# Layer 0 begun pair by pair, its second pair of images made between the passes, and group-norm statistics by batch-norm instructions: a four-layer convolution stack on one core

## The chip, the cores and the metric

The kernel runs on one core of a Trainium2 chip. The metric is the device time of one launch in microseconds. Before the change it is 3129.97 us, the median of three runs (3129.84 to 3130.12).

## What is computed

The input is four images of 32 x 32 pixels with 16 channels. Three layers of one kind follow each other, and then one of another kind; each adds its result to what it was given.

```python
def _gn(v, G=8, eps=1e-5):              # mean and variance over (32, 32, C/8) of one image
    ...
def conv(inputs, M, Wp, G):             # layers 0 to 2
    first   = einsum('ijpq,bpqc->bijc', M2, inputs)
    shifted = conv3x3(inputs, K)        # K: a 3x3x16 filter for every (i, j, f)
    diff    = relu(inputs[:, :, :, None, None, :] - shifted)
    second  = einsum('ijpq,bpqijc->bijc', W2, diff)
    return first - second
x = x + conv(_gn(x), M0, W0, G0)        # layer 0; layers 1 and 2 alike
x = x + conv(...)
x = x + conv(...)
x = x + layer3(_gn(x), ...)             # a rational filter, applied as a product with Toeplitz blocks
```

## The kernel before

**Tiling.** The 1024 output pixels of a layer, times 16 filters, are cut into NBLK = 128 blocks of 128 columns. One *unit* of work is one block of one image: ten matmul instructions at L472 (six products in two row halves: `ga` and `gb` in float32, which take two instructions each, and `gn` in float32r) fill one two-bank PSUM buffer, and one VectorE instruction at L480 (`junk`) takes the minimum with zero, multiplies with the weights `wt` and sums into `acc`. There are four PSUM buffers, so TensorE can be at most four units ahead of VectorE. A layer has 512 units, the three layers 1536.

**Order.** `conv_layer` writes the order out by hand as jobs. In layers 1 and 2 the first eight blocks are two jobs, one for images 0 and 1 and one for images 2 and 3; in layer 0 they are one job over all four images (L448). The last eight blocks are again two jobs. A chunk is GC = 8 blocks of G. `load_g` loads a chunk (`ga`, `gb` in two halves of rows each, and the broadcast `g9`); `prepare_g` subtracts on GpSimd (L400), casts `g9` to `gn` on ScalarE (L404) and forms two low parts on VectorE (L407). `load_w` (L411) loads the weights of two blocks, 1024 KB on the SP queue, as a broadcast of 8 rows to 128 partitions; only the very first such tile comes ready-made from `w0`. There are six weight buffers.

After every unit `step()` (L427) advances the generators in `todo`, so that the instructions of a generator stand between units in the order of each engine. All engines work through their instructions in the order in which they are written.

**Start of layer 0.** The host sends three shifted copies per pair of images (`raw`); `load_first(a, which, queue)` loads one of them for pair `a`, 544 KB: two into the images `ims[a][0]`, `ims[a][1]` and one into `nine[a]`. `first_images` (L168) runs the group norm on all four images, and from it makes the images in place: `center` (ScalarE, L177) subtracts the mean, `clear` (GpSimd memsets, L195) zeroes the borders, `scale` (ScalarE, L181) and `first_tap` (VectorE, L199) multiply by 1/std, and `last_tap` (VectorE, L204 to L206) makes the third image from `nine`. All four images are made before the first unit's L480. The chunk 0 of G is loaded and prepared in two parts, `halves`: blocks 0 and 1 first, blocks 2 to 7 after. The second part is prepared by the generator `rest`: its subtraction at the first step, its cast and low parts (`list(second)`, L248) at the eighth.

The SP queue carries, in this order: x, raw of pair 0, `ga`, `ga` (first part), raw of pair 1 twice, w0, the second part of chunk 0 (`ga`, `gb`, `ga`, `gb`, `g9`), weights tile 1, chunk 1 of G (1.5 MB), and further weights tiles.

**Group norm** (L104 to L145), in all layers: sum on VectorE (L110), group sum by a small matmul against `avg` (L101), mean (L114, L116), centred copy `xc` (L120), square (L125), sum (L127), group sum again, then 1/std (L132 to L144). `normalise` (L256) multiplies `xc` by 1/std. In layers 1 and 2 it runs as a generator (`make_image`) beside units, one pair at a time; before layer 3 it is `norm3` (L745), which for the second pair has the Toeplitz products of the first pair (L729) issued around its steps.

Of the kernel before, what the change touches and what calls it, by code (L numbers as in the profile page):

```python
# [37 lines left out]
P = 128  # L38
# [5 lines left out]
GC = 8  # L44
# [10 lines left out]
def conv_stack_kernel(ctx, tc, x, raw, w0, M, W, G, den, num, h0, cst, dft, one, idp, idq, perm, out):  # L55
# [40 lines left out]
    def group_sums(s):  # L96

        pt = pair_psum()
        for h in range(2):
            rows = slice(64 * h, 64 * h + 64)  # L100
            nc.tensor.matmul(pt[:, h, : s.shape[1]], lhsT=avg[rows], rhs=s[rows], start=True, stop=True)  # L101
        return [pt[:, h, : s.shape[1]] for h in range(2)]

    def group_norm(xt, center=None, sums=group_sums):  # L104


        nb = xt.shape[1]
        vec = lambda name: small.tile([P, B], F32, tag=name, name=name)[:, :nb]
        s = vec("s")
        nc.vector.tensor_reduce(s, xt, AX.X, ALU.add)  # L110
        yield
        pm = sums(s)
        mean = vec("mean")
        nc.vector.tensor_copy(mean, pm[0])  # L114
        for more in pm[1:]:
            nc.vector.tensor_tensor(mean, mean, more, ALU.add)  # L116
        if center:
            center(mean)
        xc = work.tile([P, B, NBLK], F32, tag="xc", name="xc")[:, :nb]
        nc.vector.tensor_tensor(  # L120
            xc, xt, mean.unsqueeze(2).to_broadcast([P, nb, NBLK]), ALU.subtract
        )
        sq = junkp.tile([P, S * S], F32, tag="junk", name="sq")[:, : nb * NBLK]
        sq = sq.rearrange("p (b n) -> p b n", b=nb)
        nc.vector.tensor_tensor(sq, xc, xc, ALU.mult)  # L125
        ss = vec("ss")
        nc.vector.tensor_reduce(ss, sq, AX.X, ALU.add)  # L127
        yield
        yield
        pv = sums(ss)  # L130
        v = vec("v")
        nc.vector.tensor_scalar(v, pv[0], 1e-5, None, ALU.add)  # L132
        for more in pv[1:]:
            nc.vector.tensor_tensor(v, v, more, ALU.add)

        r = vec("r")
        nc.scalar.activation(r, v, AF.Sqrt)
        ri = vec("ri")
        nc.vector.reciprocal(ri, r)
        nc.vector.tensor_tensor(ri, ri, v, ALU.mult)  # L140
        nc.vector.tensor_tensor(r, r, ri, ALU.add)
        nc.vector.tensor_scalar(r, r, 0.5, None, ALU.mult)
        rstd = vec("rstd")
        nc.vector.reciprocal(rstd, r)  # L144
        return xc, rstd  # L145

    over = lambda v: v.unsqueeze(2).to_broadcast([P, v.shape[1], NBLK])
# [20 lines left out]
    def first_images():  # L168

        of = lambda t, b: t[:, :, b % 2].rearrange("p l cc x -> p l (cc x)")  # L170
        neg = st.tile([P, B], F32, name="neg")
# [29 lines left out]
        def last_tap(b):  # L201

            v, v8, m = of(nine[b // 2], b), of(ims[b // 2][2], b), neg[:, b : b + 1]
            nc.vector.tensor_scalar(v8, v, m, rstd[:, b : b + 1], ALU.add, ALU.mult)  # L204
            nc.vector.tensor_scalar(v, v, m, rlo[:, b : b + 1], ALU.add, ALU.mult)
            nc.vector.scalar_tensor_tensor(v8, v8.bitcast(F32), sign, v, ALU.mult, ALU.add)  # L206
            clear(2, b // 2, slice(b % 2, b % 2 + 1))

        first = prepare_g(0, 0, halves[0])

        def early(mean):
            nc.vector.tensor_scalar(neg, mean, -1.0, None, ALU.mult)
            center(0, 0, 1)
            clear(0, 0)
            next(first)

        norm = group_norm(xs, early)
        while True:
            try:
                next(norm)  # L220
            except StopIteration as end:
                xc, rstd = end.value
# [6 lines left out]
        last_tap(0)  # L229
        list(first)  # L230
        scale(1)
        center(0, 2, 3)
        clear(0, 1)
        first_tap(1)
        last_tap(1)
        center(1, 2, 3)
        clear(1, 1)
        for b in (2, 3):
            scale(b)
            first_tap(b)  # L240
            last_tap(b)

        def rest():
            second = prepare_g(0, 0, halves[1])
            next(second)
            for _ in range(6):
                yield
            list(second)  # L248
            yield
            for a in range(2):  # L250
                normalise(a, xc[:, 2 * a : 2 * a + 2], rstd[:, 2 * a : 2 * a + 2])
                yield
# [3 lines left out]
    def normalise(a, xc, rstd):  # L256
        yc[a] = work.tile([P, 2, NBLK], F32, tag=f"yc{a}", name=f"yc{a}")
        nc.vector.tensor_tensor(yc[a], xc, over(rstd), ALU.mult)

    def make_image(a, xt):  # L260

        xc, rstd = yield from group_norm(xt[:, 2 * a : 2 * a + 2])
        store_image(a, xc, rstd)
# [3 lines left out]
    def store_image(a, xc, rstd):  # L267
        split = lambda t: t.rearrange("p b (cc q) -> p b cc q", q=S)
        whole, hi, lo = (ys[a][:, k, :, :, 1:33] for k in range(3))
        normalise(a, xc, rstd)  # L270
# [163 lines left out]
    def conv_layer(layer, xt, finish, side=(), also=iter(())):  # L434
# [12 lines left out]

        jobs = [(range(GC), (0, 1)), (range(GC), (2, 3))] if layer else [(range(GC), range(B))]  # L448
        jobs += [(range(blk, blk + GC), range(B)) for blk in range(GC, NBLK - GC, GC)]
        jobs += [(last, (0, 1)), (last, (2, 3))]  # L450
        for job, (blks, batches) in enumerate(jobs):
            pairs = layer and job < 2, job >= len(jobs) - 2
            for k, blk in enumerate(blks):
# [8 lines left out]
                if (job or not layer) and k == 6:  # L462
# [27 lines left out]
                if not any(pairs) and layer + job:  # L490
# [157 lines left out]
    with tc.tile_pool(name="st", bufs=1) as st:  # L648
# [17 lines left out]
        load_first(1, 0, nc.sync)  # L666
        load_first(1, 1, nc.sync)
        load_first(1, 2, nc.gpsimd)
# [3 lines left out]
        list(load_g(0, 1))  # L672
        load_w()
        first_images()
        load_w()
# [69 lines left out]
    def norm3(a, xt):  # L745
        stats = []

        def column_sums(s):
# [4 lines left out]
            pt = stats[0][:, column_sums.n, :nb]  # L753
# [4 lines left out]
            return [pt]  # L758
# [19 lines left out]
        xc, rstd = yield from steps  # L778
        if a:
            run(early[2])  # L780
        for y in (
# [3 lines left out]
            nc.vector.tensor_tensor(  # L785
                y.rearrange("p cc q b -> p b cc q"),
                xc.rearrange("p b (cc q) -> p b cc q", q=S),
                over(rstd).rearrange("p b (cc q) -> p b cc q", q=S),
                ALU.mult,
            )  # L790
# [175 lines left out]
```

## Time and profile before

| | us |
|---|---|
| median of three runs | 3129.97 |
| the profiled execution | 3129.71 |
| span of its profile, first to last instruction | 3127.8 |
| TensorE busy in it | 3109.3 |
| VectorE busy | 2069.8 |
| ScalarE busy | 82.2 |
| GpSimd busy | 233.4 |

The profile's page gives for each engine its busy time and its share of the span. A group line names the source line, the engine, the operation and the tiles, written as output<-inputs. In the timeline each row has a start, a length, the engine and the line; a bracket at its end says how long the engine had been idle before it and what ended that idle time. `PEld` is TensorE's loading of stationary operands, which overlaps its matmuls. The windows give the busy time of each engine in a stretch, and after it TensorE's granted clock, the mean busy share of the 16 DMA engines and the rate in GB/s.

### The profile page before, as it was taken

What the parts mean: (1) busy time and instruction counts of PE and PEld (TensorE: products, weight loads), DVE (VectorE), ACT (ScalarE), POOL (GpSimd) and SP (SyncE); (2) the same over time, 40 slices, a digit from 0 to 9 for tenths busy, and PEclk for the clock granted to TensorE, in tenths of its full rate; (3) what the DMA queues carried; (4) which work ended last, traced back from release to release, by engine and by line L of the source; (5) the groups of instructions that cost most, each with busy time, mean ns of one, the idle gap of its engine ahead of it and who ended that gap; (6) DMA issues with size and microseconds to landing.
All of it is one profiled execution on the core that took longest, in us unless ns stands there. A gap on an engine that the chain in (4) does not pass through costs nothing.

```text
span 3127.8 us, 39384 instructions
## 1 busy us (share of the span) xinstructions
PE 3109.3 (99%) x16312; PEld 1703.7 (54%) x16312; DVE 2069.8 (66%) x3318; ACT 82.2 (3%) x107; POOL 233.4 (7%) x259
## 2 busy tenths in 40 slices
PE   8999999999999999999999999999999999999999
PEld 4445567777777554455445455455455454455444
DVE  7666666666667766666666666766666666666663
ACT  1000000000000000000000000000000000000000
POOL 1002321000000100100000000010010000000000
PEclk9999999999999999999999999999999999999999
DMA  6553344333342665433333343266544444444511
GB/s 192 150 119 91 87 115 111 98 88 87 97 98 69 129 148 123 99 86 87 98 98 88 87 97 98 68 131 148 127 106 101 99 105 106 102 97 106 112 38 22
DMA packets 67599, 321.35 MB, mean 103 GB/s; under 512 B 10058, under 2 KB 17100, under 8 KB 41948
## 3 DMA queue, kind: packets, MB, share of 16 engines
q1 hardware_dynamic: 56776, 300.62, 40.1%
q10 hardware_dynamic: 6484, 10.81, 1.7%
q0 software_dynamic: 4160, 7.40, 1.2%
q8 instruction: 128, 2.10, 0.3%
q14 instruction: 51, 0.42, 0.1%
HBM read 313.16 MB, written 5.63 MB: 102 GB/s over the span
## 4 chain that ended last, share of the span: by engine, by line
PE 99%; DVE 1%; DMA 0%; POOL 0%; issue 0%; ACT 0%; DVEq 0%; POOLq 0%
PE pt L472 96%; PE pt L729 2%; PE pt L326 1%; DVE junk L480 0%; DMA gb<-in_G_dram 0%; PE pt L525 0%; PE pt L568 0%; DMA cs<-in_cst_dram 0%; PE pt L607 0%; POOL im L195 0%; PE pt L101 0%; DVE x L495 0%; DVE s L110 0%; PE pt L314 0%; ACT im L181 0%
## 5 line engine op out<-in xcount | busy, mean ns | idle before, releaser
L480 DVE SCALAR_TENSOR_TENSOR junk<-pt,w 128x1024 f32<-128x1024 f32 x1536 | 1880.9, 1225 | 992.8 <-PE pt L472 973.9
L472 PE MATMUL pt<-im,ga 64*128 64x512 f32 x6144 | 1679.4, 591 | 3.1 <-POOL ga L400 3.1
L472 PE MATMUL pt<-im,gb 64*128 64x512 f32 x6144 | 1671.7, 588 | 0.7 <-ACT im L181 0.7
L472 PE MATMUL pt<-im,gn 64*128 64x512 f32 x3072 | 1345.9, 806 | 0.0
L472 PEld LDWEIGHTS pt<-im,gb 64*128 64x128 f32 x6144 | 687.5, 185 | 655.9 <-issue 575.4
L472 PEld LDWEIGHTS pt<-im,ga 64*128 64x128 f32 x6144 | 680.4, 187 | 378.6 <-DVE junk L480 230.1
L472 PEld LDWEIGHTS pt<-im,gn 64*128 64x128 f32 x3072 | 356.1, 186 | 325.6 <-issue 286.7
L400 POOL TENSOR_TENSOR ga<-ga,cs 128x1024 f32<-128x1024 f32 (+2 forms) x49 | 113.5, 2317 | 2119.2 <-DMA ga<-in_G_dram 2118.1
L480 DVE DVE_READ_ACCUMULATOR junk<-pt,w 128x1 f32 x1536 | 127.4, 83 | 0.0
L407 DVE TENSOR_TENSOR gn<-g,gn 32x1024 fp32r<-32x1024 f32 (+2 forms) x98 | 120.4, 1229 | 5.1 <-ACT gn L404 3.0
L404 ACT CAST gn<-g 128x1024 fp32r<-128x1024 f32 (+2 forms) x49 | 50.4, 1029 | 2348.7 <-DMA g<-in_G_dram 2086.4
L350 POOL DMA_DIRECT2D fd<-ft x48 | 25.1, 530 | 231.0 <-DVE ft L343 213.5
L860 DVE TENSOR_TENSOR xo<-xo,pt 32x512 f32<-32x512 f32 x5 | 3.4, 682 | 35.8 <-PE pt L729 35.7
L729 PE MATMUL pt<-t,y 128*32 128x512 f32 (+3 forms) x352 | 24.3, 433 | 0.8 <-DVE xo L860 0.8
L326 PE MATMUL pt<-mt,yt 128*64 128x512 f32 x96 | 21.9, 598 | 0.0
L729 PEld LDWEIGHTS pt<-t,y 128*32 128x32 f32 x352 | 11.9, 110 | 13.5 <-issue 9.9
L292 POOL DMA_DIRECT2D im<-img x32 | 16.2, 513 | 8.9 <-DMA img<-y 8.8
L326 PEld LDWEIGHTS pt<-mt,yt 128*64 128x64 f32 x96 | 6.3, 136 | 13.7 <-issue 9.4
L729 PE MATMUL pt<-t,yp 128*32 128x512 f32 (+3 forms) x192 | 13.4, 434 | 0.0
L546 POOL TENSOR_TENSOR H<-H,d 128x256 f32<-128x256 f32 (+1 forms) x10 | 8.2, 822 | 68.1 <-DVE d L551 67.7
L275 POOL COPY e<-y 32x612 f32<-32x612 f32 x4 | 2.8, 692 | 120.6 <-DVE y L274 120.6
L546 POOL TENSOR_TENSOR t<-s 128x256 f32<-128x256 f32 (+1 forms) x15 | 11.3, 755 | 0.0
(94 smaller groups left out, 209.6 us busy)
## 6 DMA issues: line engine op xcount, KB each, us to landing
w<-in_W_dram SPq DMA_DIRECT2D x191, 1024.0 KB
ga<-in_G_dram SPq DMA_DIRECT2D x94, 256.0 KB
gb<-in_G_dram SPq DMA_DIRECT2D x94, 256.0 KB
g<-in_G_dram SPq DMA_DIRECT2D x47, 512.0 KB
mt<-in_M_dram SPq DMA_DIRECT2D x24, 512.0 KB
t<-hd ACTq DMA_DIRECT2D x28, 160.0 KB
t<-hd SPq DMA_DIRECT2D x28, 160.0 KB
im<-img SPq DMA_DIRECT2D x32, 67.5 KB
```

What stands on the lines that cost most here:

```text
L275: nc.gpsimd.tensor_copy(ye[a][96:, :, :, 1:, :], ys[a][96:, :, :, :3, :])
L292: (nc.sync, nc.scalar, nc.gpsimd)[n % 3].dma_start(out=ims[a][k][at : at + C] .bitcast(F32) .rearrange("c l b cc x -> c l (b cc x)")[:, :, ...
L326: nc.tensor.matmul(pf[64 * h : 64 * h + 64], lhsT=yt[:, 4 * part + k].rearrange("k b c -> k (b c)"), rhs=mts[k][:, h, :], start=(k == 0), ...
L350: nc.gpsimd.dma_start(out=fv[h, cc, b], in_=ft[at : at + C, cc])
L400: nc.gpsimd.tensor_tensor(gv, gv, mid.unsqueeze(1).to_broadcast([P, gv.shape[1], C]), ALU.subtract)
L404: nc.scalar.copy(gn, g9)
L407: nc.vector.tensor_tensor(lo, g9[r : r + 32], lo.bitcast(F32), ALU.subtract)
L472: nc.tensor.matmul(pt[:, half, :], lhsT=w[rows, blk % GC, :], rhs=im[rows, :, b % 2, :, :S], start=n == 0, stop=n == 2,)
L480: nc.vector.scalar_tensor_tensor(junk, pt.rearrange("p h m -> p (h m)"), 0.0, wt, ALU.min, ALU.mult, accum_out=acc[b // 2][:, b % 2, blk : ...
L546: mul = lambda o, u, w: nc.gpsimd.tensor_tensor(o, u, w, ALU.mult)
L729: nc.tensor.matmul(rows[:, :, r], lhsT=lhsT, rhs=rhs, start=at not in begun, stop=left[at] == 0)
L860: nc.vector.tensor_tensor(row, row, src, ALU.add)
```

## The change

Layer 0 now begins like the other layers, with two jobs for the first eight blocks: images 0 and 1, then images 2 and 3. The raw copies of pair 1 are all loaded on the SP queue, behind weights tiles 1 and 2. Chunk 1 of G is loaded inside the first job. The images of pair 1 are made by `rest`, between units: the cast and low parts of the second part of chunk 0 at the second step, centring and clearing of pair 1 at the third, image 2 at steps 8 to 11, image 3 at steps 12 to 15, and `normalise` at 16 and 17. In all layers the statistics come from VectorE's `bn_stats`, one instruction per image, which gives means and squared deviations of even and odd elements; three small instructions form the group's squared deviation, and no centred copy is kept. `normalise` and the end of `norm3` become one two-scalar instruction per image.

```diff
     def group_norm(xt, center=None, sums=group_sums):
-        s = vec("s")
-        nc.vector.tensor_reduce(s, xt, AX.X, ALU.add)
+        st = small.tile([P, B, 2, 3], F32, tag="st", name="st")[:, :nb]
+        for b in range(nb):
+            nc.vector.bn_stats(st[:, b].rearrange("p e k -> p (e k)"), xt[:, b])
+        half, m, m2 = NBLK // 2, st[:, :, :, 1], st[:, :, :, 2]
         yield
-        pm = sums(s)
-        mean = vec("mean")
-        nc.vector.tensor_copy(mean, pm[0])
-        for more in pm[1:]:
-            nc.vector.tensor_tensor(mean, mean, more, ALU.add)
+        pm, axes = sums(m)
+        neg = vec("neg")
+        nc.vector.tensor_reduce(neg, pm, axes, ALU.add)
+        nc.vector.tensor_scalar(neg, neg, -float(half), None, ALU.mult)
         if center:
-            center(mean)
-        xc = work.tile([P, B, NBLK], F32, tag="xc", name="xc")[:, :nb]
-        nc.vector.tensor_tensor(
-            xc, xt, mean.unsqueeze(2).to_broadcast([P, nb, NBLK]), ALU.subtract
-        )
...
-        nc.vector.tensor_tensor(sq, xc, xc, ALU.mult)
-        ss = vec("ss")
-        nc.vector.tensor_reduce(ss, sq, AX.X, ALU.add)
+            center(neg)
+        d = small.tile([P, B, 2], F32, tag="d", name="d")[:, :nb]
+        nc.vector.tensor_tensor(d, m, neg.unsqueeze(2).to_broadcast([P, nb, 2]), ALU.add)
+        nc.vector.tensor_tensor(d, d, d, ALU.mult)
+        nc.vector.scalar_tensor_tensor(d, d, float(half), m2, ALU.mult, ALU.add)
...
-        first = prepare_g(0, 0, halves[0])
+        first, second = (prepare_g(0, 0, part) for part in halves)
...
         first_tap(0)
         nc.vector.tensor_scalar(rlo, rstd, is_lo, None, ALU.mult)
-        last_tap(0)
+        list(last_tap(0))
         list(first)
         scale(1)
-        center(0, 2, 3)
-        clear(0, 1)
         first_tap(1)
-        last_tap(1)
-        center(1, 2, 3)
-        clear(1, 1)
-        for b in (2, 3):
-            scale(b)
-            first_tap(b)
-            last_tap(b)
+        list(last_tap(1))
+        next(second)
 
         def rest():
-            second = prepare_g(0, 0, halves[1])
-            next(second)
-            for _ in range(6):
-                yield
+
+            yield
             list(second)
             yield
+            for which in range(2):
+                center(which, 2, 3)
+                clear(which, 1)
+            yield
+            for _ in range(4):
+                yield
+            for b in (2, 3):
+                scale(b)
+                first_tap(b)
+                yield
+                yield from last_tap(b)
+                yield
             for a in range(2):
...
-        jobs = [(range(GC), (0, 1)), (range(GC), (2, 3))] if layer else [(range(GC), range(B))]
+        jobs = [(range(GC), (0, 1)), (range(GC), (2, 3))]
...
-            pairs = layer and job < 2, job >= len(jobs) - 2
+            pairs = job < 2, job >= len(jobs) - 2
...
         next(loads)
         next(loads)
-        load_first(1, 0, nc.sync)
-        load_first(1, 1, nc.sync)
-        load_first(1, 2, nc.gpsimd)
         load_w()
         list(loads)
         load_w()
-        list(load_g(0, 1))
+        load_w()
+        for which in range(3):
+            load_first(1, which, nc.sync)
         load_w()
         first_images()
-        load_w()
```

`last_tap` yields after each of its first two VectorE instructions. `normalise` becomes, per image, `tensor_scalar(yc[a][:, b], xt[:, b], neg[:, at], rstd[:, at], ALU.add, ALU.mult)`.

## The prediction

> **What bounds the kernel now.** I read the page's busy times first, then the chain of work that ended last in order of time, then what TensorE waits for, then the timeline of the first 60 us and of the ends of the layers.
>
> ```profile
> PE 3109.3 (99%) x16312; PEld 1703.7 (54%) x16312; DVE 2069.8 (66%) x3318; ACT 82.2 (3%) x107; POOL 233.4 (7%) x259
> ```
>
> TensorE is busy for all but 18.5 us. Nothing in the change takes a matmul away from L472, so it can win only in those 18.5 us, and lose wherever TensorE is made to wait. The waits it has:
>
> ```profile
> PE pt L101 <- DVE s L110: 6.9, 6, 4.9
> PE pt L472 <- POOL ga L400: 3.1, 1, 3.1
> PE pt L101 <- DVE ss L127: 3.0, 2, 2.7
> PE pt L472 <- ACT im L181: 0.7, 2, 0.4
> ```
>
> Columns: us in total, times, longest. The longest ones are the start; what is left is about 0.4 us at each of five pair ends. The start, from the timeline:
>
> ```profile
> 11.06 0.72 POOL L400 TENSOR_TENSOR ga<-ga,cs 128x256 f32<-128x256 f32 x1 [1.02 <-DMA gb<-in_G_dram]
> ...
> 19.56 1.06 PE L472 MATMUL pt<-im,ga 64*128 64x512 f32 x4
> ...
> 20.98 1.13 PE L472 MATMUL pt<-im,gb 64*128 64x512 f32 x4 [0.36 <-ACT im L181]
> ...
> 24.14 1.04 PE L472 MATMUL pt<-im,ga 64*128 64x512 f32 x4
> ...
> 27.58 0.83 ACT L404 CAST gn<-g 128x768 fp32r<-128x768 f32 x1 [6.01 <-DMA g<-in_G_dram]
> ...
> 31.59 1.93 DVE L407 TENSOR_TENSOR gn<-g,gn 32x768 fp32r<-32x768 f32 x2
> ...
> 35.66 1.23 DVE L480 SCALAR_TENSOR_TENSOR junk<-pt,w 128x1024 f32<-128x1024 f32 x1 [0.54 <-DMA w<-in_W_dram]
> ...
> 39.03 2.36 POOL L400 TENSOR_TENSOR ga<-ga,cs 128x1024 f32<-128x1024 f32 x1 [14.31 <-DMA ga<-in_G_dram]
> ```
>
> ```profile
> 52.33 1.23 DVE L480 SCALAR_TENSOR_TENSOR junk<-pt,w 128x1024 f32<-128x1024 f32 x1 [3.18 <-DMA w<-in_W_dram]
> ```
>
> Three things are to be seen. The first matmul waits for a piece of chunk 0 that lands at 11.06. The third unit starts at 19.56 and the fifth at 24.14; the rows after repeat every 1.963 us (26.11, 28.07, 30.03), so two periods from 19.56 would give 23.49: image 2 cost 0.65. And three brackets date landings: the second part of `g9` at 27.58, weights tile 1 at 35.66, tile 2 at 52.33. Tile 2 came 3.18 us late for VectorE, and TensorE did not stop: four PSUM buffers cover nearly three units.
>
> ```profile
> 4.00:8.00 4.00, 0.59 (x4) 0.51 (x4) 3.03 (x7) 0.33 (x1) 0.00 (x0) 1.00 1.03 402
> 12.00:16.00 4.00, 3.71 (x10) 1.44 (x10) 2.89 (x7) 2.60 (x5) 1.39 (x8) 1.00 1.02 418
> 28.00:34.00 6.00, 6.00 (x35) 3.23 (x34) 5.70 (x9) 0.41 (x1) 0.00 (x0) 1.00 0.52 130
> 70.00:78.00 8.00, 8.00 (x42) 4.06 (x40) 5.57 (x9) 0.00 (x0) 0.00 (x0) 1.00 0.51 211
> ```
>
> The last two columns are the DMA engines' share and GB/s. While raw copies move, all 16 engines are busy at 402 to 418. While only a weights tile moves, half of them are, at 130: 35.66 - 27.58 = 8.1 us per tile. Later (70 to 78) a tile runs at 211, 5.0 us.
>
> [...] The weights' source has 8 outermost, and the share of 0.52 agrees. [...] `ga` of chunk 1, queued on SP behind tile 1, let L400 start only at 39.03, after tile 1. [...] rows here agree (4 elements 161 ns, 256 elements 426, 512 elements 691). [...]
>
> **The change, part by part.** *Start, first two units.* The piece awaited at 11.06 stands ahead of pair 1's raw copies on its queue before and after, so I put nothing there; the earlier 1/std buys nothing either, since memsets and L400 come later. Third unit without image 2's wait: **-0.65**. TensorE's undisturbed schedule is then unit n at 19.56 + 1.963(n-3): unit 5 at 23.49, 9 at 31.34, 13 at 39.19, 17 at 47.04, 19 at 50.97.
>
> *What the transfers allow.* The first job has two images instead of four, so half as much work covers each transfer: the second part of G is due at unit 5 instead of 9, tile 1 at 5, tile 2 at 9, tile 3 at 13: one per 4 units, 7.85 us, against 8.1 us to move one. Pair 1's raw copies (3 x 544 KB = 1.67 MB at 402 to 418 GB/s: 4.1 us, 1.37 each) no longer stand ahead of these. So `g9` lands at 27.58 - 4.1 = 23.5, tile 1 at 35.66 - 4.1 = 31.6, tile 2, right behind, at 39.7. Half of each raw copy lies on the weights' engines, behind tile 2: 41.1, 42.4, 43.8. Tile 3: 51.9.
>
> *Second part of chunk 0.* The cast runs 23.5 to 24.35, L407 to 26.3. Unit 5's `gn` product is due 1.32 after its start (24.14 to 25.46 before): 24.81. Wait **1.5**. It pushes unit 9 to 32.85. VectorE starts unit 5's L480 with tile 1 at 31.6 and ends at 32.85, which frees unit 9's buffer just then: tile 1 hides behind the same wait.
>
> *Images 2 and 3.* VectorE works in order, and `first_tap(2)` stands before unit 9's L480, so a late raw copy holds all units behind it. The first copy lands at 41.1; two L177 (1.39), five memsets (0.93 to 1.21, I take 1.2), 43.7 with hand-overs; L199 0.50, 44.2; unit 9's L480 ends at 45.45, and only then has TensorE a buffer for unit 13, due at 39.19. Total wait so far **6.2**. This, not the weights, is the latest arrival; tile 2 at 39.7 alone would have cost 1.8. From 44.2 VectorE does four units (1.335 each with the accumulator read: 5.3) and the rest of image 2 (0.56 + 0.57 + 0.79 with gaps 2.0): 51.5; `first_tap(3)` 52.0, with tile 3 there; units 13 to 15 and `last_tap(3)`, 6.0: 58.0; memsets 0.35. Image 3 is whole at 58.4; unit 18, at 45.45 + 5 x 1.963 = 55.3, wants it 1.32 later, at 56.6: **1.8** more. Altogether 8.0 of wait. Pair 1's job reuses the four tiles, and chunk 1 (1.5 MB behind tile 3, some 9 us as before from 35 to 44) lands near 61, due near 87: nothing more is lost.
>
> *Statistics.* At a pair's end the order is L495, L110, then L101, for which TensorE waits:
>
> ```profile
> 3044.32 0.42 DVE L110 TENSOR_REDUCE s<-x 128x2 f32<-128x256 f32 x1
> ...
> 3044.89 0.39 PE L101 MATMUL pt<-s,cs 64*128 64x2 f32 x4 [0.44 <-DVE s L110]
> ```
>
> Two `bn_stats` of 128 elements take its place. [...] 0.29 each, so 0.29 + 0.03 + 0.29 - 0.42 = 0.2 later. Bounds: 0.16 each, the smallest row, 0.07 earlier; two passes, 0.42 each, 0.46 later. Six times (five pair ends, and the last, where the Toeplitz products end just as the sum is ready): **+1.2** (-0.4 to +2.8). Three small instructions (0.16) replace L120, L125 and L127 (0.43 each), 0.8 less: in layer 2's first pair TensorE has 0.33 of idle for the second sum and loses its overlap besides (2.78 between units against about 2.10 in the other layers): **-0.6**. Elsewhere the second sum comes with no wait, and nothing is won. One two-scalar instruction per image instead of a 0.43 product per pair lies in VectorE's 0.7 us of idle per unit.
>
> *Sum.* -0.65 + 8.0 + 1.2 - 0.6 = +7.95 on the profiled execution's 3129.71 (its span and 1.9 around it, 0.26 under the median): 3137.7; beside the median 3137.9. I take **3137.8**.
>
> **Rivals.** *Quick weights.* If tiles 1 and 2 run at the later 211 GB/s, tile 1 lands at 28.5, tile 2 at 33.5, the first copy at 34.9; `first_tap(2)` ends at 38, unit 9's L480 at 39.3, before unit 13 (40.7 with the wait for `gn`). What remains is 1.5 - 0.65 + 0.6: 3131.2, not slower by what can be measured. It decides at about 6 us a tile. For it: the row at 70 to 78; against: tile 1 follows the same transfer as before, which took 8.1. *Everything arrives in time*: the start's 0.65 stays won and `bn_stats` is at its lower bound: 3129.71 - 0.65 - 0.4 - 0.6 = 3128.1. Against it stands the order on SP. *Slower still*: 9 us a tile (tile 2's stretch, 43.8 to 52.3, had 8.5) brings unit 13 to 47.3, 1.9 more, and two-pass statistics 1.6 more: 3141.3 and above.
>
> **How the numbers follow.** A measurement of this kernel can tell about 0.2%, 6.3 us, from no change: slower means above 3136.2. Late transfers as worked out, 3134.5 to 3140.5: 0.60, four fifths of it above the line. Quick weights 0.22, in time 0.08, slower still 0.10. Slower 0.48 + 0.10 = 0.58; within 0.41; faster 0.01, since only 18.5 us are idle at all. The range 3130.5 to 3141 leaves out the case in time and most of the slowest.
>
> **What would show it.** In the profile after: VectorE's L404/L407 pair near 24 with TensorE waiting on it; an L480 waiting for `w` near 31; `first_tap` idle until about 43.7 because of ScalarE or GpSimd waiting for `in_raw`; TensorE's idle time up by some 8 us before 60 us, and L101's waits near 0.6 at each pair's end. It is wrong if raw copies of pair 1 land before 36, or if TensorE's units run through the first 60 us without a break.

## The result, and the profile after

The changed kernel takes **3143.38 us** (median of five runs, 3142.89 to 3143.89), the kernel before beside it 3129.97: a ratio of 1.0042, 95% interval 1.003 to 1.0054. It is slower by 13.4 us where 8 had been forecast, and above the range. The profiled execution took 3143.76 with a span of 3142.0, that is 14.2 more than the span before.

The page's busy times, and what TensorE waits for in the profile after (us in total, times, longest):

```profile
PE 3114.9 (99%) x16312; PEld 1538.1 (49%) x16312; DVE 2067.3 (66%) x3338; ACT 82.3 (3%) x107; POOL 231.5 (7%) x258
```

```profile
PE pt L477 <- DVE junk L485: 7.8, 2, 4.4
PE pt L103 <- DVE st L114: 7.3, 6, 5.0
PE pt L477 <- POOL ga L406: 4.6, 1, 4.6
PE pt L103 <- DVE d L126: 1.1, 1, 1.1
...
PE pt L477 <- DVE gn L413: 0.7, 2, 0.5
...
PE pt L477 <- POOL im L191: 0.2, 1, 0.2
```

The matmul of the units is now L477, VectorE's instruction of a unit L485, the group sum L103, `center` L173, `clear` L191 and `first_tap` L195. New is the first row: twice TensorE had no free PSUM buffer because VectorE stood. L413, the low parts of `gn`, is the wait that was forecast for unit 5. TensorE is also busy 5.6 us longer with the same 16312 instructions. Where the first row comes from is dated by the brackets in the timeline of the first 65 us:

```profile
23.14 0.83 ACT L410 CAST gn<-g 128x768 fp32r<-128x768 f32 x1 [8.28 <-DMA g<-in_G_dram]
...
24.00 1.93 DVE L413 TENSOR_TENSOR gn<-g,gn 32x768 fp32r<-32x768 f32 x2 [3.61 <-ACT gn L410]
...
35.52 1.22 DVE L485 SCALAR_TENSOR_TENSOR junk<-pt,w 128x1024 f32<-128x1024 f32 x1 [6.99 <-DMA w<-in_W_dram]
36.81 2.08 PE L477 MATMUL pt<-im,ga 64*128 64x512 f32 x4 [4.42 <-DVE junk L485]
...
46.55 2.83 ACT L173 ACTIVATE im<-im,neg 128x544 f32<-128x544 f32 x4 [22.58 <-DMA im<-in_raw_dram]
...
48.95 0.50 DVE L195 TENSOR_SCALAR im<-im,rstd 128x544 f32<-128x544 f32 x1 [8.19 <-POOL im L191]
50.65 1.13 PE L477 MATMUL pt<-im,ga 64*128 64x512 f32 x4 [3.41 <-DVE junk L485]
...
59.09 1.22 DVE L485 SCALAR_TENSOR_TENSOR junk<-pt,w 128x1024 f32<-128x1024 f32 x1 [3.01 <-DMA w<-in_W_dram]
...
64.37 0.31 POOL L191 MEMSET im<- 128x16 f32 x2 [9.41 <-DVE im L204]
...
64.56 0.69 PE L477 MATMUL pt<-im,gn 64*128 64x512 f32 x2 [0.18 <-POOL im L191]
...
64.91 1.19 PE L477 MATMUL pt<-im,ga 64*128 64x512 f32 x4
```

The last row is the start of unit 19, which in the profile before is this row:

```profile
51.63 1.04 PE L472 MATMUL pt<-im,ga 64*128 64x512 f32 x4
```

VectorE stood 6.99 us for weights tile 1, which landed at 35.4, and so TensorE 4.42 at unit 9. It stood 8.19 for `first_tap(2)` (L195), that is for GpSimd's borders and before them for ScalarE's centring (L173), which waited for the raw copy until 46.55; so TensorE waited 3.41 at unit 13. Tile 3 landed at 59.0, and image 3, whose last parts are queued on VectorE behind units that need tile 3, was whole at 64.7. Unit 19, which started at 51.63 before, starts at 64.91: 13.3 us later. From the chain of work that ended last (start, length, what):

```profile
2.91 11.97 DMA w<-in_w_dram
17.66 41.31 DMA w<-in_W_dram
59.09 1.23 DVE junk L485 x2
60.72 1.22 DVE junk L485 x2
62.33 1.22 DVE junk L485 x2
64.56 43.88 PE pt L477 x200
```

The program's end hangs on tile 3: queued on SP at 17.66 behind the other loads of the start, landed 41.31 later. The windows (busy time of PE, PEld, DVE, ACT, POOL; then the granted clock, the DMA engines' share, GB/s) show at which rate it all came:

```profile
24.00:28.00 4.00, 3.27 (x16) 1.97 (x13) 3.83 (x5) 0.00 (x0) 0.00 (x0) 1.00 0.97 150
28.00:35.00 7.00, 4.38 (x23) 3.17 (x20) 0.53 (x2) 0.00 (x0) 0.00 (x0) 0.98 0.74 121
35.00:45.00 10.00, 8.19 (x30) 3.90 (x32) 4.93 (x8) 0.00 (x0) 0.00 (x0) 0.67 0.57 118
45.00:50.00 5.00, 2.24 (x14) 0.85 (x10) 1.05 (x2) 2.78 (x4) 1.19 (x8) 1.00 0.64 212
50.00:59.00 9.00, 8.35 (x34) 4.01 (x36) 6.08 (x12) 1.39 (x2) 0.70 (x5) 0.81 0.50 116
```

From 24 to 28 all engines are busy (0.97), and only 150 GB/s arrive, where 402 to 418 had come with all of them busy before: a busy DMA engine can be a slow one. In the other stretches in which weights move, with half to three quarters of the engines busy, it is 116 to 121, not the 130 that the forecast had beside its 8.1 us a tile. The three tiles took 12.3 us (23.1 to 35.4), 9.9 (to 45.3) and, behind the raw copies, which were in at 49.5, 9.5 (to 59.0). And the clock column has a thing that the prediction overlooked: around its waits TensorE's clock was halved, from 34.7 to 41.6 and from 51.8 to 55.2, which is where most of its 5.6 us more of busy time lie.

A pair's end with the new statistics:

```profile
1026.73 0.49 DVE L114 BATCH_NORM_STATS2 st<-x 128x6 f32<-128x128 f32 x2
...
1027.37 0.39 PE L103 MATMUL pt<-st,cs 64*128 64x4 f32 x4 [0.44 <-DVE st L114]
```

Two `bn_stats` take 0.49 together where the sum had taken 0.42, and TensorE waits 0.44 as before.

### The profile page after: what moved, and what is told of

Same layout as the page of the kernel before. It is cut to its first block, busy times and chain, and to the rows that moved or that the text cites. A ratio compares the mean times of both kernels' runs of the same rounds, so it can differ in the third digit from the quotient of the medians.

```text
span 3142.0 us, 39397 instructions
## 1 busy us (share of the span) xinstructions
PE 3114.9 (99%) x16312; PEld 1538.1 (49%) x16312; DVE 2067.3 (66%) x3338; ACT 82.3 (3%) x107; POOL 231.5 (7%) x258
## 4 chain that ended last, share of the span: by engine, by line
PE 96%; DMA 3%; DVE 1%; SPq 0%; issue 0%; ACT 0%; ACTq 0%; POOL 0%; DVEq 0%; POOLq 0%
PE pt L477 94%; PE pt L732 1%; DMA w<-in_W_dram 1%; DMA td<-s 1%; PE pt L332 1%; DMA w<-in_w_dram 0%; DVE junk L485 0%; PE pt L530 0%; PE pt L612 0%; PE pt L103 0%; DVE x L500 0%; ACT s L581 0%; DVE st L114 0%; PE pt L320 0%; PE pt L573 0%
## 5 line engine op out<-in xcount | busy, mean ns | idle before, releaser
L485 DVE SCALAR_TENSOR_TENSOR junk<-pt,w 128x1024 f32<-128x1024 f32 x1536 | 1880.7, 1224 | 996.0 <-PE pt L477 970.8
L477 PE MATMUL pt<-im,ga 64*128 64x512 f32 x6144 | 1588.2, 591 | 12.5 <-DVE junk L485 7.8
L477 PE MATMUL pt<-im,gb 64*128 64x512 f32 x6144 | 1579.3, 589 | 0.1
L477 PE MATMUL pt<-im,gn 64*128 64x512 f32 x3072 | 1253.6, 806 | 0.9 <-DVE gn L413 0.7
L477 PEld LDWEIGHTS pt<-im,gb 64*128 64x128 f32 x6144 | 597.9, 186 | 725.1 <-issue 719.7
L477 PEld LDWEIGHTS pt<-im,ga 64*128 64x128 f32 x6144 | 598.4, 188 | 451.2 <-DVE junk L485 280.2
L477 PEld LDWEIGHTS pt<-im,gn 64*128 64x128 f32 x3072 | 300.7, 186 | 362.8 <-issue 357.9
L485 DVE DVE_READ_ACCUMULATOR junk<-pt,w 128x1 f32 x1536 | 127.8, 83 | 0.0
L413 DVE TENSOR_TENSOR gn<-g,gn 32x1024 fp32r<-32x1024 f32 (+2 forms) x98 | 121.0, 1234 | 9.1 <-ACT gn L410 7.0
L410 ACT CAST gn<-g 128x1024 fp32r<-128x1024 f32 (+2 forms) x49 | 50.4, 1029 | 2323.1 <-DMA g<-in_G_dram 2246.3
```

The lines of the kernel that those rows point to most:

```text
L410: nc.scalar.copy(gn, g9)
L413: nc.vector.tensor_tensor(lo, g9[r : r + 32], lo.bitcast(F32), ALU.subtract)
L477: nc.tensor.matmul(pt[:, half, :], lhsT=w[rows, blk % GC, :], rhs=im[rows, :, b % 2, :, :S], start=n == 0, stop=n == 2,)
L485: nc.vector.scalar_tensor_tensor(junk, pt.rearrange("p h m -> p (h m)"), 0.0, wt, ALU.min, ALU.mult, accum_out=acc[b // 2][:, b % 2, blk : ...
```

## The experiments

The kernels of one group ran on one chip beside the kernel before, whose median there was 3130.24 us for the first group, 3129.46 for the second, 3129.69 for the third and 3129.77 for the fourth.

### First group: statistics, clock, transfers

The theory: late landings, above all of weights tiles, set the time. Rivals: the half clock after the waits, and the statistics.

**Statistics alone.** Layer 0 keeps its one first job over four images and its old order of loads; only `group_norm`, `normalise` and the end of `norm3` are the new ones.

```diff
-        jobs = [(range(GC), (0, 1)), (range(GC), (2, 3))]
+        jobs = [(range(GC), (0, 1)), (range(GC), (2, 3))] if layer else [(range(GC), range(B))]
...
```

> Layer 0 is put back as it was before (one job over four images, old order of loads); only the batch-norm statistics and the two-scalar normalise stay. In the changed kernel the last part of the way, after unit 64, is 0.7 us longer than before in all. If the statistics cost what these rows show, the time is 3130 to 3131, with the start as before. If the statistics carry a good part of the loss (rival), it is above 3134.

Measured: 3129.74, ratio 1.0000 (0.9992 to 1.0008). The statistics cost nothing that can be told; the loss lies in the new beginning of layer 0.

**Waits filled.** Units 8 and 12 repeat their first product (5 and 6 times, results overwritten), so that TensorE is busy while it would have waited.

```diff
+                    fill = {(3, 1): 5, (5, 1): 6}.get((blk, b), 0) if not layer and job == 0 else 0
+                    for _ in range(fill):
+                        for half in range(2):
+                            rows = slice(64 * half, 64 * half + 64)
+                            nc.tensor.matmul(pt[:, half, :], ...)
```

> The changed kernel with 4.3 us of additional first products in unit 8 and 5.2 us in unit 12 (overwritten by the true ones), so that TensorE is not idle in the two long waits and its clock isn't halved at 34.7 to 41.6 and 51.8 to 55.2. Transfers theory: the landing of weights tile 3 near 59 us sets units 17 to 19 whatever TensorE's clock was before, so the time stays at 3143.4 within 0.6. Clock theory: the half-rate stretches cost 2.4 and 1.8 us of their own, so the time falls to about 3139.3.

Measured: 3143.85, ratio 1.0046 (1.003 to 1.0061). Its windows:

```profile
24.00:35.00 11.00, 10.52 (x54) 8.77 (x52) 3.42 (x5) 0.00 (x0) 0.00 (x0) 1.00 0.82 125
35.00:45.00 10.00, 9.09 (x47) 4.17 (x45) 4.93 (x8) 0.00 (x0) 0.00 (x0) 1.00 0.56 125
45.00:50.00 5.00, 4.89 (x24) 1.89 (x20) 1.31 (x2) 2.78 (x4) 1.25 (x9) 1.00 0.63 198
50.00:59.00 9.00, 8.12 (x40) 3.71 (x40) 6.18 (x13) 1.39 (x2) 0.64 (x5) 1.00 0.50 119
```

The clock stays at 1.00 throughout, and the time is the same: the half clock cost nothing that can be told, since the units that it slowed would have waited for the next landing anyway. The tiles land at 35.2, 45.1 and 58.5, as in the changed kernel.

**Ready-made tiles.** Weights tiles 1 to 3 come like tile 0, as 128 rows repeated by the host.

```diff
-            in_=src.unsqueeze(1).to_broadcast([8, C, 2 * S * S]) if wts else w0,
+            in_=src.unsqueeze(1).to_broadcast([8, C, 2 * S * S]) if len(wts) > 3 else w0[len(wts)],
...
```

> The changed kernel, with weights tiles 1 to 3 ready-made in memory for all 128 partitions like tile 0, so that each moves on 16 DMA engines instead of being broadcast from 8 rows on 8. Transfers theory: tile 1 lands near 26, tile 2 near 29, pair 1's raw copies near 33, tile 3 near 36; no unit waits for them, only the gn product of unit 5 (1.2 us), and the time is 3130 to 3132. If the transfers were only an accompaniment and the new order on VectorE and GpSimd is what stalls TensorE (rival), it stays above 3138.

Measured: 3130.11, ratio 1.0000 (0.9992 to 1.0008). TensorE's waits and two windows:

```profile
PE pt L103 <- DVE st L114: 7.6, 6, 5.3
PE pt L477 <- POOL ga L406: 3.9, 1, 3.9
...
PE pt L477 <- DVE gn L413: 0.5, 1, 0.5
```

```profile
22.00:24.00 2.00, 2.00 (x13) 0.97 (x9) 1.18 (x2) 0.76 (x1) 0.00 (x0) 1.00 0.97 404
24.00:26.60 2.60, 2.12 (x14) 1.58 (x11) 2.46 (x4) 0.00 (x0) 0.00 (x0) 1.00 1.01 411
```

At 404 to 411 GB/s tiles 1 and 2 land at 24.2 and 26.7, the raw copies by 30.8, tile 3 at 36.4. The wait on L485 is gone, and with it the whole 13.3 us, although the order of the work is that of the changed kernel. So the order itself costs nothing that can be told; the tiles do.

**Raw copies first.** Pair 1's raw copies stand ahead of tile 0 on the queue, as before the change.

```diff
+        for which in range(2):
+            load_first(1, which, nc.sync)
+        load_first(1, 2, nc.gpsimd)
         load_w()
         list(loads)
         load_w()
         load_w()
-        for which in range(3):
-            load_first(1, which, nc.sync)
         load_w()
```

> The changed kernel, with pair 1's raw copies back on the queues where they were before the change, ahead of tile 0; the total of bytes ahead of tile 3 is the same. If weights tiles are slow because the raw copies are read at the same time by the other engines (contention), tiles 1 to 3 take about 8 us each again after the second part of g9 at 27.6, tile 3 lands near 52, and the time is about 3136.5. If a tile takes 10 to 12 us in this place whatever else moves, tile 3 still lands near 59 and the time stays at 3142 to 3144.

Measured: 3139.74, ratio 1.0031 (1.0019 to 1.0044), between what was expected of the two. The raw copies are there at 14.7, tiles 1 to 3 land at 36.7, 46.1 and 53.0: 9.4, 9.4 and 6.9 us. Tile 2 now sets the time: 46.1 + 1.3 for L485 = 47.4 for unit 13, due at 39.2; 8.2 less the 0.65 of the start is 7.5, and the units run 7.7 late in its trace. The raw copies beside tile 1 explain some 3 us of its 12.3; without them a tile still takes longer than 8.1.

### Second group: what makes a tile slow

**No raw copies.** Leaves out the load of pair 1's raw copies; zeros stand in their tiles.

```diff
-        for which in range(3):
-            load_first(1, which, nc.sync)
+        image_tiles(1)
+        nine[1] = st.tile([P, 4, 2, 4, 34], F32, name="nine1")
+        for t in (*ims[1][:2], nine[1]):
+            nc.vector.memset(t, 0.0)
```

> Leaves out the load of pair 1's three raw copies (1.67 MB): their tiles are set to zero on VectorE at the very start, so images 2 and 3 are computed from zeros; every instruction after that is as in the changed kernel. Behind weights tiles 1 to 3 on the queue there is now only chunk 1 of G. Theory (a weights tile is slowed by what the other eight engines read meanwhile; beside chunk 1 alone a tile took 8.0 to 9.4 us): tile 1 lands at 31 to 32.5, tile 2 at 39 to 41.5, tile 3 at 46 to 50; unit 13 then starts about 3.5 us late and the time is 3132 to 3134.5. Rival (these tiles take 12.3 and 9.9 us at this place whatever lies behind them): tile 1 at 35.4, tile 2 at 45.3, and about 3137, since only the wait for image 2 goes.

Measured: 3135.51, ratio 1.0019 (1.0012 to 1.0026). Tiles at 33.4, 42.1, 50.5: 10.6, 8.7 and 8.4 us, with only chunk 1 of G beside them. Faster than with raw copies, slower than expected, and so is the time.

**Nothing beside the tiles.** As that one, and chunk 1 is held back until the second job: a one-column write by VectorE into its tiles comes ahead of its load.

```diff
+        if at == (0, 1):
+            for t in (ga, gb, g9):
+                nc.vector.memset(t[:, 0, :1], 0.0)
...
-                if k == (3 if job == 0 else 1):
+                if k == 1 and (layer or job):
...
```

> Pair 1's raw copies left out as in the run without them (zeros in their place), and chunk 1 of G held back until the second job has begun, so that no transfer of the queue runs beside weights tiles 1 to 3. Theory (slowed by the neighbours' reads): about 6.9 us a tile, as tile 3 of the raw-first run had with nothing beside it: tile 1 at 30, tile 2 at 37, tile 3 at 44, TensorE waits only for gn (about 1.2 us), and the time is 3130.4 (3129.5 to 3131.5). Rival (the neighbours do not matter, only the eight engines' own rate): 8 to 9.4 us a tile, as without the raw copies, and 3132 to 3134.5.

Measured: 3137.02, ratio 1.0023 (1.0013 to 1.0032), and no faster tiles: 30.4, 39.4, 49.1, that is 9.1, 9.0 and 9.7 us. Its windows over the three tiles:

```profile
23.00:30.00 7.00, 7.00 (x38) 4.10 (x36) 3.51 (x6) 3.06 (x5) 1.64 (x11) 1.00 0.52 118
31.00:39.00 8.00, 7.24 (x36) 3.68 (x38) 4.83 (x9) 0.00 (x0) 0.00 (x0) 1.00 0.51 117
40.00:48.00 8.00, 7.18 (x36) 3.62 (x38) 6.25 (x12) 0.00 (x0) 0.26 (x2) 1.00 0.50 117
```

117 GB/s with half of the engines and nothing beside them: **here the theory of the neighbours fell**. A neighbour makes a tile slower still (tile 1 took 12.3 us beside raw copies and 10.6 beside chunk 1, for 9.1 here), but these tiles are slow alone. (Of the time, 2.4 and 0.9 us arose at the starts of layers 1 and 2, whose second chunk this edit moved too.)

**Row by row.** Tiles 1 to 3 in eight transfers each, one source row to 16 partitions.

```diff
+        if 0 < len(wts) < 4:
+            for r in range(8):
+                nc.sync.dma_start(out=flat[r * C : (r + 1) * C], in_=src[r : r + 1].to_broadcast([C, 2 * S * S]))
...
```

> The changed kernel with weights tiles 1 to 3 loaded in eight transfers each, one per source row, every one a broadcast of that row to 16 partitions; nothing left out and no array added. Theory (a tile is slow because its eight outermost rows put it on eight engines): with sixteen outermost copies all sixteen engines carry it; eight issues of about 0.6 us limit it to some 5 us a tile, tile 1 lands by 28, tile 2 by 32, the raw copies by 34, tile 3 by 40; the time is that of the ready-made tiles, 3130.1 (3129.3 to 3131). Rival (slow because the same row of memory is read sixteen times): it stays at 8 us and more a tile and the time at 3137 or above.

Measured: 3137.20, ratio 1.0025 (1.0015 to 1.0035). Its windows, while tiles 1 and 2 move:

```profile
24.00:28.00 4.00, 3.11 (x17) 1.97 (x13) 3.83 (x5) 0.00 (x0) 0.00 (x0) 1.00 0.87 148
28.00:33.00 5.00, 5.00 (x28) 4.29 (x26) 2.93 (x6) 0.00 (x0) 0.00 (x0) 1.00 0.90 121
```

Nine tenths of all sixteen engines are busy, and they bring 121 GB/s: the number of engines is not the limit either. That fell too; what was left was the rival, one row read sixteen times.

**The same with `g9` first.** In the second part of chunk 0, `g9` is loaded ahead of `ga` and `gb`.

```diff
+            if at == (0, 0) and part.start:
+                g9_part()
             for half in range(2):
...
```

> The row-by-row kernel, and in the second part of chunk 0 the broadcast g9 ahead of ga and gb instead of behind them. Theory: g9 lands near 19.5 instead of 23, the cast and low parts are done before unit 5 asks for them at 24.8, and the last wait for gn (0.5 us with ready-made tiles) goes: 3129.6 (3128.8 to 3130.4), which is at the edge of what can be told from the kernel before. Rival: ga and gb of the second part now land later and GpSimd's subtraction becomes what unit 5 waits for: 3130.1 or more.

Measured: 3139.57, ratio 1.0032 (1.0019 to 1.0044). The rival held: `g9` at 21.4, but `ga` and `gb` at 26.3 instead of 18.1, and unit 5 waits 4.8 us for GpSimd's subtraction.

### Third group: the same row again and again?

**Nothing beside the tiles, again**, with the chunk of layers 1 and 2 where the changed kernel has it.

```diff
-                if k == (3 if job == 0 else 1):
+                if k == (3 if job == 0 else 1) and (layer or job):
...
```

> As the run in which nothing lay beside the tiles (pair 1's raw copies left out, zeros in their place, chunk 1 held back), but layers 1 and 2 load their second chunk at the third block as the changed kernel does, where that run had moved it to the first by mistake and lost 2.4 and 0.9 us at the starts of these layers. Tiles of about 9 us again (9.0 to 9.7, packets of 560 to 590 ns), tile 3 near 49; unit 17 then waits until 50.3 instead of starting at 47.0, and the time is 3.3 us above the kernel before plus 0.6 in the later layers: some 4 us above it (3 to 5). If the tiles land as before and the time is still 7 us above, the loads of layers 1 and 2 were not the reason and the sum from landings fails.

Measured: 3130.88, ratio 1.0005 (0.9996 to 1.0013), 1.2 us above the kernel before and not 3 to 5. But single runs spread from 3128.8 to 3133.8, and the profiled one, at 3133.79, is the slowest of them. In its trace the forecast holds: the tiles take 9.2, 9.1 and 9.8 us (117 to 120 GB/s), and its units run 3.7 us late from layer 0 on, and 4.1 at the start of layer 2. So the moved chunks were the reason for the rest. The other runs have no trace; that their tiles were quicker is the likeliest reading of the spread, and not shown.

**Eight engines, different rows.** Tiles 1 to 3 from rows repeated by the host, with a seventeenth row between them, which keeps eight outermost pieces and eight engines, but lets no row be read twice.

```diff
+                else w0[128 + 136 * len(wts) - 136 :][:136].rearrange("(r c) m -> r c m", r=8)[:, :C] if wts else w0[:128]
...
```

> The changed kernel with weights tiles 1 to 3 from rows that the host has repeated (16 copies each, a seventeenth row left between them so that the transfer keeps eight outermost rows and with them eight engines). Theory (the tiles are slow because the same 8 KB are read again and again; eight engines alone would carry 211 GB/s): packets of about 311 ns, 5.0 us a tile, tile 1 at 28.3, tile 2 at 33.3, raw copies at 34.7 to 37.4, tile 3 at 42.4; the time 0 to 1.5 us above the kernel before, as my rival of quick weights had it. Rival (slow because eight engines carry it, whatever they read): 12.3, 9.9 and 9.5 us a tile again, and 13.4 us above the kernel before.

Measured: 3143.39, ratio 1.0040 (1.0025 to 1.0055), the time of the changed kernel, with 116 to 131 GB/s. So reading one row again is not it. Eight engines with distinct rows are slow (116 GB/s at 36 to 45), sixteen with one row are slow (121), sixteen with ready-made rows are quick (404 to 411). What the slow ones have in common lies at the *destination*: by the layout of their loads, which is all there is to go by, since no trace shows where a packet is written, they fill it in whole blocks of 16 partitions.

### Fourth group: how the destination is dealt out, and the step of the engines

The theory of this group was a guess of the author's, about a way into SBUF that no trace shows: engines that fill blocks of partitions in step, all at the same place in their blocks, hold each other up, and some packets apart they do not. It was sized from what had been measured: 573 to 598 ns for 8 KB in the first tiles with nothing beside them, against 313 to 316 in the ready-made ones, about twice. A weights tile of eight rows shows in a trace as 128 pieces of 8 KB, called packets here, and eight reports of an engine's end; that each engine fills one block of 16 partitions, one packet to a partition, is the author's reading of the layout.

**Blocks of eight.** Sixteen engines, eight neighbouring partitions to each by the layout; rows repeated by the host.

```diff
+                else w0[128 + 144 * len(wts) - 144 :][:144].rearrange("(r c) m -> r c m", r=16)[:, :8] if wts else w0[:128]
...
```

> The changed kernel with weights tiles 1 to 3 from rows that the host has repeated, two spare rows left in every eighteen so that the transfer has sixteen outermost pieces of eight rows: sixteen engines, and engine r writes the eight partitions from 8r on, where the ready-made tiles (313 ns a packet) let the transfer be split as its 128 rows are. Theory, [...] a packet takes about twice 311, some 560 to 620 ns, a tile about 4.9 us; [...]. Rival (the slowness comes with eight engines or with one source row, which are both absent here): 313 ns, 2.4 us a tile, as with the ready-made tiles. Time: the theory 0 to 1.5 us above the kernel before (tile 1 near 28, tile 2 near 33, raw copies to 37, tile 3 near 42), the rival within 0.5 of it, so that the packets decide and not the time.

Measured: 3132.83, ratio 1.0009 (1.0000 to 1.0017). Its windows over tiles 1 and 2, the first of which is in 4.5 us after the last of `g9`:

```profile
25.00:28.00 3.00, 1.84 (x5) 1.33 (x7) 2.83 (x5) 0.00 (x0) 0.00 (x0) 0.76 0.99 216
28.00:33.00 5.00, 5.00 (x23) 4.14 (x22) 3.96 (x7) 0.00 (x0) 0.00 (x0) 0.80 0.99 218
```

All engines busy and 216 to 218 GB/s, half of the 404 to 411 of the ready-made tiles with as many engines and rows as distinct. Packets of 611 ns in tile 2, against 313. The rival is out. The time is 1.6 above what was expected; TensorE's wait for `gn` was 2.3 us, for `g9` had landed at 23.8.

**Out of step.** Two small loads into a scratch tile ahead of tile 1, of six and of two outermost pieces, put the engines of rows 0 and 1 ten packets, those of rows 2 to 5 five packets behind those of rows 6 and 7. The tiles themselves are loaded as in the changed kernel.

```diff
+        shift = st.tile([P, 2 * S * S], F32, name="shift")
+        rows = W[0][0, :, 2:4, :].rearrange("p k m -> p (k m)")
+        for n, at in ((6, 0), (2, 64)):
+            nc.sync.dma_start(
+                out=shift[at : at + 5 * n],
+                in_=rows[:n].unsqueeze(1).to_broadcast([n, 5, 2 * S * S]),
+            )
         load_w()
         load_w()
```

> The changed kernel with two small extra loads ahead of weights tile 1 on the queue, into a scratch tile: 6 x 5 and 2 x 5 rows of 8 KB, six and then two outermost pieces, so that the engines of rows 0 and 1 start the tile ten packets later than those of rows 6 and 7 and those of rows 2 to 5 five packets later. Nothing left out. Theory [...]: packets of tiles 1 to 3 near 311 ns where no other transfer is beside them, 311 to 600 beside the raw copies; tile 1 lands at 31 to 33.5 in spite of 3.1 us for the extra loads, tile 2 5 to 6 us later, tile 3 before 48; the time 1 to 4 us above the kernel before instead of 13.4. Rival (it is not the step of the engines): packets of 600 and more as in the changed kernel, everything 3 us later than there, 3146 and more.

Measured: 3138.88, ratio 1.0030 (1.0018 to 1.0041). The windows in which tiles 1 and 2 come:

```profile
26.00:30.00 4.00, 4.00 (x25) 3.43 (x21) 0.89 (x2) 0.00 (x0) 0.00 (x0) 1.00 0.76 164
30.00:34.00 4.00, 0.74 (x5) 0.10 (x1) 0.00 (x0) 0.00 (x0) 0.00 (x0) 1.00 0.64 195
34.00:38.00 4.00, 1.85 (x4) 0.84 (x6) 2.93 (x5) 0.00 (x0) 0.00 (x0) 0.50 0.64 209
```

The same tiles on the same eight engines now come at 195 to 209 GB/s (some 160 of it weights, by the count of their packets, the rest copies on the other engines), where 117 had been with nothing beside them. The median packet of tile 2 takes 320 ns. Of the landings and the time the forecast was wrong: the extra loads took longer than thought, the last of them being in at 27.9, 6.4 us after `g9` where 3.1 had been reckoned, so that tile 1 landed at 34.7, over an us later than the latest that was expected; tile 2 followed after 7.7 us, not 5 to 6, since the engines that had been put back end it and a part of the packets is still slow; tile 3 landed at 54.5 instead of before 48; and 9.1 us were lost instead of 1 to 4. The packets speak for the theory, the time only against the rival's 3146. The tiles' loads read the same source rows as in the changed kernel, so that the source is not what made the difference.

The packets of the first weights tiles, each tile's median time in ns from the traces' packet records (128 packets of 8 KB a tile):

```
kernel                 tile 1  2    3    4    5    6    7
before                 572   525  485  388  354  311  312
changed                777   613  612  516  454  412  591
nothing beside         573   593  598  579  686  542  545
row by row             716   998  888   (eight rows again from tile 4)
eight engines          872   607  588   (distinct rows)
blocks of eight        650   611  634
ready-made             641   313  316
out of step            477   320  320  374  313  320  322
```

(Tile 1 is mixed everywhere with packets of `g9`'s time.) The medians lie at three levels: 311 to 320 (ready-made and out of step in tiles 2 and 3, the kernel before in tile 6), 573 to 634 where eight or sixteen engines fill blocks of partitions and little else moves, and 888 to 998 row by row, where by the layout the sixteen engines of a transfer fill one block of 16 partitions. That these are about one, two and three times 313 is measured; why was not shown. The rates agree with the medians: at 8 KB for each engine in a median, eight engines at 573 ns would carry 114 GB/s, sixteen at 611, 313 and 998 ns 215, 419 and 131 (an estimate from the table), and 117, 216 to 218, 404 to 411 and 121 were measured.

Whether engines were in step can be read from the traces too, which record when each of the eight engines of a tile reports its end. In the changed kernel these eight ends lie within 0.5 us of each other in tiles 1 and 2, and within 0.6 in the runs with nothing beside the tiles and with different rows. Out of step, tile 1 ends on two engines at 30.4 to 30.9, on four at 32.3 to 33.1 and on two at 34.5 to 34.7: the groups stayed apart. And the kernel before has both states: from tile 1 to tile 6 the ends spread from 0.8 over 1.6 and 1.9 to 2.0 us, over six packets of 311, while the median packet falls from 572 to 311. Its engines had drifted apart. That is the window at 211 GB/s of the prediction, and its 130 was a mixture.

So it is shown that these tiles are slow while their engines are in step, 593 to 613 ns a packet in tile 2 (nothing beside, eight engines, changed) against 320 out of step, and that the source is not the reason (607 with distinct rows). What engines in step share, and which partitions would share it, was not shown.

## Why the prediction was wrong

**Right:** the sign, the order of events and where they would show. Image 2 no longer holds the units at the start, which is the 0.65 of the forecast: from the third unit to the fifth it is 3.92 us, where it was 4.58. Another 0.64, which the forecast did not have, had come by the third unit, as unit 2 started 0.24 earlier and the clock was up at 17.7 instead of 18.7 (in the traces here it comes anywhere from 14.9 to 18.7, so that this part may be chance). It was worth nothing, since landings set what follows. `g9` landed at 23.1 (23.5), L404/L407, now L410/L413, ran at 23 to 26, and unit 6 starts 1.2 late for it (1.5). The raw copies took 1.2, 1.4 and 1.6 us (1.37 each) behind tile 2. `first_tap(2)` held VectorE, because of the raw copy and not of the weights, as said. Chunk 1 came in time.

**The step that failed** is "35.66 - 27.58 = 8.1 us per tile". The tiles took 12.3, 9.9 and 9.5 us. Tile 3 was put at 51.9 and landed at 59.0: -0.4 from `g9`, +4.2 and +1.8 from tiles 1 and 2, +0.1 from the raw copies, +1.4 from tile 3 itself, 7.1 in all. The forecast let the end of this stretch hang on VectorE's work behind the raw copy, with tile 3 just in time; in the run the same work began 5.2 us later (48.95 for 43.7) and VectorE then stood another 3.01 for tile 3. What follows from the landings was sized rightly: image 3 is whole 6.3 us later than forecast (64.7 for 58.4), and at unit 32 the work runs 13.4 late where 7.35 had been forecast, 6.1 more. With ready-made tiles, where this term is gone, the loss is gone.

Why the number was wrong: it was one difference of two landings, taken as a rate of the transfer ("half of them are, at 130"). It is a rate of a state. The prediction had the other state before its eyes, 211 GB/s at 70 to 78 with the same share of engines, and used it only for a rival, with no reason why it came and went. With its engines in step and nothing beside it a tile takes 9.0 to 9.8 us, and 12.3 when raw copies move as well. That a tile of eight rows moves on eight engines, on which I leant, is right (a share of 0.50 to 0.52 with nothing beside it) and was not what bound: sixteen engines brought 121 GB/s. What bounds these tiles is known only as far as the step of their engines. That raw copies, which other engines move meanwhile (a share of 0.97 from 24 to 28), slow tile 1 was shown by leaving them out (packets of 632 ns for 777) and by loading them ahead (614 for the 870 of the run with filled waits, both on one chip); by what way they do so was not shown. "Pair 1's raw copies no longer stand ahead" had been counted as a gain of 4.1 us, and that they now move beside tile 1 had been put at nothing: it cost 1.7 to 2.9 us of tile 1, as 12.3 stands to the 10.6 without raw copies and the 9.4 with them ahead.

**Statistics.** +1.2 was too much: 0.07 at each end of a pair instead of 0.2. One `bn_stats` took 0.28, as the estimate of 0.29 had it (the rows of 256 and 512 elements before, 426 and 691 ns, come to 0.29 when continued to 128), but the second follows after 0.21 us. The -0.6 in layer 2's first pair is there (0.53 between units 1520 and 1530). In the trace about 0.5 us are lost around units 205 to 225 of layer 0, where the chain of work runs over ScalarE's copy at L581 and the stores `td<-s` behind it, and about 0.4 at the end, neither of which was looked into further; the statistics alone measured -0.5 +- 2.5.

**Of the rivals**, "slower still" came nearest, with 9 us a tile, but was sized at 3141.3 with two-pass statistics that did not come; it had 0.10. "Quick weights" is what the blocks of eight are, at 4.5 to 4.8 us a tile: +3.1 measured, +1.2 forecast, the difference being the wait for `gn`.

**No version beat both kernels**: the best, the statistics alone and the ready-made tiles, are as fast as the kernel before as far as can be told.

## What to carry to other kernels

A transfer's rate read from one pair of landings is a sample: look at the same transfer elsewhere in the trace, and if it has two rates, find what separates them before using either. When a change halves the work that covers a chain of transfers, the margin is gone, and a tenth more per transfer adds up along the chain. For a broadcast into blocks of partitions, look at how far apart its engines end (0.5 us in tile 2 of the changed kernel, at 613 ns a packet; 2.0 us in tile 6 of the kernel before, at 311); here distinct sources left a packet at 588 to 607 ns in tiles 2 and 3, and more engines at 611 to 998, where ready-made tiles had 313 to 316.

## What the runs showed of the hardware

- With nothing beside it, a DMA of eight blocks of 16 partitions moved 117 to 120 GB/s, at a median of 573 to 623 ns per 8 KB, while its eight engines ended within 0.4 to 1.3 us of each other. On the same engines some packets apart the median was 320 ns (out of step, ends 4.3 and 6.1 us apart in tiles 1 and 2) and 311 (kernel before, tile 6, ends 2.0 us apart). In the run out of step it lasted: 322 ns still in tile 7.
- Sixteen busy engines can mean 121 GB/s (row by row), 217 (blocks of eight) or 408 (ready-made): the DMA share shows occupation, not flow.
- In two waits of 4.4 and 3.4 us TensorE's clock fell to half, once within the wait and once 1.1 us after it, and stayed there for 6.8 and 3.4 us. Here it cost nothing that can be told: with the waits filled and the clock at 1.00 the time was 3143.85 for 3143.38.
- `bn_stats` on 128 x 128 float32 takes 0.28 us, two of them 0.49.
